# A state-space layer and a binarised MLP on one core: the scan's channels interleaved in pairs, smaller buffers, sums in groups of the array, and new transfer durations in the planner

## The chip, the cores and the metric

The kernel runs on 1 core of one Trainium2 chip. The time is that of the device, in microseconds (us), from the start of the program to its end. A profile is one more execution, with its own time. The engines of the core: PE multiplies matrices, DVE (VectorE) and POOL (GpSimd) work element by element, ACT (ScalarE) computes functions and copies, SP issues nearly all transfers. All five run their own instruction queue in order and wait for each other through semaphores.

## The reference, cut to what matters

Eight images x of 384 channels and 1024 positions go through a state-space block; then an MLP with weights reduced to signs is added. All is float32.

```python
t = layernorm(layernorm(x))                     # over channels
xm, z = split(t @ in_proj_w.T)                  # 768 channels each
xc = silu(causal_conv3(xm) + conv_b)
dt, Bm, Cm = split(xc @ x_proj_w.T, [24, 40])   # ranks 24, 16, 16
dt = softplus(dt @ dt_proj_w.T + dt_proj_b)
dA = exp(dt * A)                                # 16 states a channel
h[l] = dA[l] * h[l-1] + dt[l] * xc[l] * Bm[l]   # along 1024 positions
y = (sum over states of h * Cm) + xc * D
t = (y * silu(z)) @ out_proj_w.T
x = x + gelu(t @ mlp_w1.T + mlp_b1) @ mlp_w2.T + mlp_b2
# then, with sign-reduced W1, W2 and a clip per group of images:
x = x + quant(gelu(quant(layernorm(x) @ sign(W1))) @ sign(W2))
```

The last step quantises per group of one image for the first five images; for the other three it contributes zero, so they skip it.

## The kernel before, in words

Every operation is first written down in a `Plan` (L163), with its engine, a duration in us, what it reads and writes, and a priority; `run` (L221) then emits them one by one. It simulates the five engines, takes the engine that can start first, and there the operation of the best `rank` (L256) whose buffers are free. The order of each engine's queue, and so of all transfers on SP, comes from these durations. For a transfer, L332 to L334 reckon one shared stream: 1.0 us after the issue, 395 KB a us, and 0.9 us until it has landed. Where PE would be idle for more than 0.7 us (L312), `fill` (L412) issues filler products into the tile "spare", which compute nothing. Buffers come from rings (L369 to L386), one tag each, with a fixed number of tiles.

`s1` (L598) makes, image by image and in two halves of 512 positions, xc (p_in, L648), the product dbc with dt's 24 rows and B and C (p_dbc, L690; it yields two partial sums that lie on partitions 0 to 63 and 64 to 127), B and C added up and stored (p_bc, L701 to L716), dt in six products of the full array (p_dt, L722), softplus in one instruction over 3072 elements, dt times xc on POOL (L732), and z. xc, z, dt and dtx go to DRAM, each with one store of 1.5 MB a half, because the scan needs each channel on four partitions, one for each of four states.

`scan` (L761) takes 12 units an image. A unit has two tiles of 32 channels by four states and 1024 positions, and four quads of states. The first and the last image are scanned in halves, so a tile there is twice 512. For every tile and quad, `scan_tile` (L870) lets ACT compute da = exp(dt * A) into PSUM, POOL multiply dtx by B into u (L886), DVE run the recurrence (L890), and either POOL (L904) or DVE (L907) multiply by C; `on_pool` (L866) gives POOL 11 of 24 tiles. PE then adds the four states of a channel with a matrix of 32 columns, `fold`; four such products with outputs on four groups of 32 partitions make one slot of the array (L842). The result, gated by z, goes to DRAM.

`s3` (L912) does the out projection and the first MLP (p_out, p_h, p_o); gelu runs over 3072 elements at a time. `ffn` (L1092) is the second MLP (p_y twice), with the hidden layer stored and loaded again for the maximum that its clip needs. `binarise` (L988) reduces W1 and W2 to signs once, near the start; its means come from 21 products with a matrix of ones (p_sums, L1018). `mlp_out` (L977) takes the hidden layer in two parts of six chunks. For the last image `s3` follows the scan at once, with yg kept on chip.

Of the kernel before, what the change touches and what calls it, by code (L numbers as in the profile page):

```python
# [26 lines left out]
F32 = mybir.dt.float32  # L27
# [6 lines left out]
P = 128  # L34
# [8 lines left out]
HK = KH // 2  # L43
T = 512
# [42 lines left out]
def c_act(n):  # L87
    return 0.25 + n * 0.00084
# [5 lines left out]

def c_pool(n):
    return 0.18 + n * 0.00214
# [33 lines left out]
class Piece:  # L130
# [8 lines left out]

    def __getitem__(self, part):  # L140
        return self, part

# [13 lines left out]
class Op:  # L156
    __slots__ = (
        "engine", "cost", "emit", "prio", "slack", "table", "size",
        "wants", "next", "ready", "tiles", "others", "settle",
# [3 lines left out]
class Plan:  # L163
# [12 lines left out]
    def add(self, engine, cost, emit, r=(), w=(), claim=(), table=None, size=0, others=None):  # L176
# [3 lines left out]
        op.size, op.prio = size, (*self.prio, len(self.ops))  # L180
# [40 lines left out]
    def run(self):  # L221
# [60 lines left out]
        while left:  # L282
# [49 lines left out]
            if e == "SP":  # L332
                dma_free = max(dma_free, end + 1.0) + op.size / 395e3
                end = dma_free + 0.9  # L334
# [17 lines left out]
class Layer:  # L352
    def __init__(self, ctx, tc, a, out):
# [9 lines left out]
        def ring(tag, bufs, where=sbuf):  # L363
# [7 lines left out]
            "front": ring("front", 2), "t_f": ring("t_f", 2), "w_f": ring("w_f", 3),  # L371
            "dbc": ring("dbc", 1), "halo": ring("halo", 2),

            "dt_r": ring("dt_r", 3), "dtx_r": ring("dtx_r", 3), "u": ring("u", 9),
# [4 lines left out]
            "yg": ring("yg", 1), "hid": ring("hid", 2), "t_b": ring("t_b", 1), "w_b": ring("w_b", 3),  # L379
            "w6": ring("w6", 2), "w6_n": ring("w6_n", 2), "res": ring("res", 2),  # L380

            "t_n": ring("t_n", 2), "small": ring("small", 7),
# [9 lines left out]
        for b in range(B):  # L392
            for name in ("dt", "dtx"):
                self.dram[name, b] = handed(f"{name}_d{b}", [DI, L])
# [24 lines left out]

    def constants(self):
# [13 lines left out]
        self.pick = const.tile([P, 2 * NS], F32, name="pick")  # L436
        nc.vector.tensor_add(self.pick, ident[:, DQ : 2 * DQ], ident[:, DP + DQ : DP + 2 * DQ])
        self.edge = const.tile([P, KD, 2], F32, name="edge")
# [23 lines left out]
    def load(self, to, view, src, r=(), size=0, cost=0.4):  # L462

        self.plan.add(
            "SP", cost, lambda: self.nc.sync.dma_start(view(to.real), src), r=r, w=[to],
            size=size,
        )

    def store(self, dst, frm, view, w, size, cost=0.4):
# [6 lines left out]
    def rows_moved(self, t, parts, move, r, w):  # L476
        n = P // len(parts)
        for i, mem in enumerate(parts):
            self.plan.add(
                "SP", 0.35, lambda i=i, mem=mem: move(t.real[i * n : (i + 1) * n, :], mem),  # L480
# [3 lines left out]
    def weights(self, ring, k, src, r=()):  # L484
        w = self.piece(ring, [P, k, P], ring)
        self.load(w, lambda t: t, src, r=r, size=4 * P * k * P, cost=0.34)
        return w

    def matmuls(self, p, w, t, k0, n, start, stop, r, claim, w0=0):


        def emit():
            for k in range(n):
                self.nc.tensor.matmul(  # L494
                    p.real, w.real[:, w0 + k, :], t.real[:, k0 + k, :],
# [776 lines left out]
```

## Time and profile before

| what | us |
|---|---|
| median of 3 runs (lowest, highest) | 3261.21 (3260.56, 3263.69) |
| the profiled execution | 3262.23 |
| its span, first to last instruction | 3260.4 |
| mean clock granted to PE | 0.984 of full |
| busy: PE, DVE, ACT, POOL | 3122.5, 2742.3, 2024.3, 2848.7 |
| transfers | 748.73 MB, 230 GB/s |

In the lists, a row is a group of equal instructions: line, engine, operation, output and inputs by name, shapes and count, then the busy time of the group (overlaps counted once), the mean duration of one in ns, and the idle time of the engine just before them with what ended most of it. A float32 product shows as two matrix records, so 1152 records are 576 products. In rows of waits come the total, the number of times and the longest. In rows of stretches come the stretch and its length, then for PE, its weight loads, DVE, ACT and POOL the busy time and number of records, then the clock, the share of the transfer engines and GB/s.

### The profile page before, as it was taken

To read this page: it belongs to the slowest core of one execution; us is meant where nothing else is said; L and a number is where in the kernel's file an instruction comes from. 1 tells how busy PE (TensorE), PEld (TensorE's weight loads), DVE (VectorE), ACT (ScalarE), POOL (GpSimd) and SP (SyncE) were. 2 spreads that over 40 slices of the span, in tenths; PEclk is the share of its full clock that TensorE was granted. 3 is DMA by queue.
4 is the path that set the end of the run, shared out by engine and by line. 5 is a ranking of instruction groups with operands and counts; after the bars stand their busy time and mean duration, and the time that the engine had idled before them with its cause. 6 is when DMAs were issued, how large, how long until landed. Compare 5 with 4: busy or idle time off the path is not lost.

```text
span 3260.4 us, 34027 instructions
## 1 busy us (share of the span) xinstructions
PE 3122.5 (96%) x11098; PEld 1317.7 (40%) x11098; DVE 2742.3 (84%) x2127; ACT 2024.3 (62%) x2246; POOL 2848.7 (87%) x1371
## 2 busy tenths in 40 slices
PE   8988999999999999999899999999999999999999
PEld 4333433444433434334334344343443534433334
DVE  4778899799978899888998878999788988789880
ACT  4778787656665576665656566755666565656551
POOL 1688899979999989999989999989999899999970
PEclk9998999999999999999999999999999999999999
DMA  6988778657796568675686667866677656766542
GB/s 218 305 282 276 249 250 294 221 183 234 259 322 197 184 230 291 229 238 197 208 298 211 237 211 246 295 225 226 220 275 250 207 185 205 249 187 207 167 141 76
DMA packets 367345, 748.73 MB, mean 230 GB/s; under 512 B 33856, under 2 KB 111168, under 8 KB 367168
## 3 DMA queue, kind: packets, MB, share of 16 engines
q1 hardware_dynamic: 366736, 746.46, 68.5%
q8 instruction: 89, 1.46, 0.2%
q14 instruction: 88, 0.72, 0.1%
q10 hardware_dynamic: 432, 0.09, 0.0%
HBM read 566.06 MB, written 180.36 MB: 229 GB/s over the span
## 4 chain that ended last, share of the span: by engine, by line
PE 74%; DMA 9%; DVE 6%; ACT 5%; issue 2%; POOL 2%; SPq 1%; ACTq 0%; DVEq 0%; POOLq 0%
PE p_y L494 17%; PE p_o L494 14%; PE p_h L494 13%; PE py L842 9%; PE p_out L494 6%; PE p_z L494 6%; PE p_in L494 5%; DVE da L890 2%; DMA w<-in_out_proj_w 2%; DMA w_f<-in_in_proj_w 2%; DVE u L890 1%; ACT L510 1%; DMA w_b<-in_mlp_w 1%; ACT da L510 1%; PE spare L412 1%
## 5 line engine op out<-in xcount | busy, mean ns | idle before, releaser
L886 POOL TENSOR_TENSOR u<-dtx_r,bc 128x1024 f32<-128x1024 f32 x768 | 1790.4, 2362 | 72.3 <-DMA dtx_r<-dtx_d 46.3
L510 ACT ACTIVATE da<-dt_r,a_neg 128x1024 f32<-128x1024 f32 (+1 forms) x960 | 902.7, 945 | 534.0 <-DVE u L907 331.1
L904 POOL TENSOR_TENSOR u<-u,bc 128x1024 f32<-128x1024 f32 x352 | 828.4, 2364 | 121.5 <-DVE u L890 115.5
L890 DVE TENSOR_TENSOR_SCAN da<-da,u 128x1024 f32<-128x1024 f32 (+1 forms) x416 | 840.5, 2020 | 111.6 <-POOL u L886 62.9
L890 DVE TENSOR_TENSOR_SCAN u<-da,u 128x1024 f32<-128x1024 f32 (+1 forms) x352 | 699.5, 2010 | 90.3 <-ACT da L510 63.0
L494 PE MATMUL p_h<-t,w_b 128*128 128x512 f32 x1152 | 513.6, 600 | 10.9 <-DMA w_b<-in_mlp_w 9.9
L907 DVE TENSOR_TENSOR u<-da,bc 128x1024 f32<-128x1024 f32 x416 | 507.9, 1221 | 10.5 <-ACT state L901 0.3
L494 PE MATMUL p_o<-g,w 128*128 128x512 f32 x1152 | 506.7, 595 | 5.4 <-ACT g L510 2.9
L842 PE MATMUL py<-u,fold 128*32 128x512 f32 x3072 | 376.6, 605 | 4.5 <-DVE u L907 4.5
L494 PEld LDWEIGHTS p_h<-t,w_b 128*128 128x128 f32 x1152 | 214.7, 190 | 298.1 <-issue 256.4
L494 PEld LDWEIGHTS p_o<-g,w 128*128 128x128 f32 x1152 | 215.9, 190 | 292.0 <-issue 277.3
L494 PE MATMUL p_y<-tn,w_b 128*128 128x512 f32 x720 | 324.9, 598 | 4.0 <-DVE tn L592 3.3
L494 PE MATMUL p_y<-gf,w_n 128*128 128x512 f32 x720 | 319.0, 599 | 6.7 <-DMA w_n<-bin_w 4.0
L510 ACT ACT_TABLE_LOAD x222 | 284.8, 1283 | 11.7 <-DVE xc L661 7.3
L494 PE MATMUL p_out<-yg,w 128*128 128x512 f32 x552 | 249.2, 604 | 8.9 <-DMA w<-in_out_proj_w 4.3
L494 PE MATMUL p_z<-t,w_f 128*128 128x512 f32 x504 | 232.5, 611 | 8.2 <-DMA w_f<-in_in_proj_w 6.2
L494 PE MATMUL p_in<-t,w_f 128*128 128x512 f32 x504 | 228.3, 602 | 10.8 <-DMA w_f<-in_in_proj_w 8.6
L494 PEld LDWEIGHTS p_y<-gf,w_n 128*128 128x128 f32 x720 | 135.1, 191 | 187.6 <-issue 172.4
L494 PEld LDWEIGHTS p_y<-tn,w_b 128*128 128x128 f32 x720 | 133.9, 190 | 183.9 <-issue 155.4
L842 PEld LDWEIGHTS py<-u,fold 128*32 128x32 f32 x3072 | 81.5, 110 | 261.1 <-issue 203.2
L525 ACT ACTIVATE g<-p_h,v_vecs 128x512 f32<-128x512 f32 x157 | 106.3, 681 | 120.9 <-PE p_h L494 120.7
L525 ACT ACTIVATE y<-p_y,v_vecs 128x512 f32<-128x512 f32 x138 | 94.1, 683 | 130.0 <-PE p_y L494 100.3
(112 smaller groups left out, 2700.3 us busy)
## 6 DMA issues: line engine op xcount, KB each, us to landing
dtx_r<-dtx_d SPq DMA_DIRECT2D x144, 512.0 KB, 5.8
dt_r<-dt_d SPq DMA_DIRECT2D x144, 512.0 KB, 6.0
w_b<-in_mlp_w SPq DMA_DIRECT2D x192, 192.0 KB, 2.9
w<-in_mlp_w SPq DMA_DIRECT2D x96, 384.0 KB, 3.6
w_f<-in_in_proj_w SPq DMA_DIRECT2D x168, 192.0 KB, 4.2
y_d<-y SPq DMA_DIRECT2D x120, 256.0 KB, 3.4
gf<-y_d SPq DMA_DIRECT2D x20, 1536.0 KB, 9.5
xc_d<-xc SPq DMA_DIRECT2D x16, 1536.0 KB, 7.3
```

What stands on the lines that cost most here:

```text
L412: self.plan.fill = lambda: self.nc.tensor.matmul(self.plan.spare.real[:, : 2 * P], self.ones, self.one.to_broadcast([P, 2 * P]), start=Tru ...
L494: self.nc.tensor.matmul(p.real, w.real[:, w0 + k, :], t.real[:, k0 + k, :], start=start and k == 0, stop=stop and k == n - 1,)
L510: lambda: self.nc.scalar.activation(out(), in_(), func, **{k: v() if callable(v) else v for k, v in kw.items()}),
L525: nc.scalar.activation(out(), in_(), AF.Identity, bias=bias, scale=scale)
L842: nc.tensor.matmul(py.real[p0 : p0 + DQ, :], self.fold, hc, start=False, stop=(q == NQUAD - 1), skip_group_check=True,)
L886: add("POOL", 2.36, lambda: nc.gpsimd.tensor_mul(u.real, dtx_r.real, spread(bq)), r=[dtx_r, bq], w=[u])
L890: add("DVE", (0.2 if half else 0.15) + n * 0.00209, lambda k=k, col=col: nc.vector.tensor_tensor_scan(to.real[:, k, :], da.real[:, k, :], ...
L904: add("POOL", 2.36, lambda: nc.gpsimd.tensor_mul(u.real, u.real, spread(cq)), r=[cq], w=[u])
L907: add("DVE", 1.21, lambda: nc.vector.tensor_mul(u.real, da.real, spread(cq)), r=[da, cq], w=[u])
```

## The change

- **Pairs.** A scan unit holds two groups of 32 channels whose elements alternate in memory, [position, channel of the pair]. `scan_tile` becomes `scan_pair`: one POOL product for both channels of a pair, with the row of B or C repeated within a pair of elements (step 0), recurrences that read and write every second element, and fold products that do so too. s1 makes dtx interleaved (three POOL products a half instead of six) and stores it so; one load brings both channels. `on_pool` now decides for pairs: quads 0 and 2 always, quad 1 in every fourth unit, 27 of 48 pairs. In the last quad u takes the place of dtx. The ring of u has three pairs instead of nine tiles, that of dtx two pairs instead of three tiles. The assignment of channels to partitions (`_laid_out`) follows.
- **Pieces of two chunks.** xc, z, dt, yg and the hidden layers are `Split` into pieces of 2 x 512 elements with buffers of their own; silu, softplus, gelu, clips, stores and loads go piece by piece, and `mlp_out` emits its products two at a time. The first piece of an in-place function waits for all parts.
- **Sums in groups of the array.** One product with a matrix `join` adds dbc's two partial sums and puts dt's rows on partitions 0 to 31 and again on 32 to 63, B and C behind them; it is evicted into dbc. dt's products then run in twos, on rows 0 to 31 and 32 to 63 of the array, into two PSUM tiles. B and C leave with one store instead of four. In `binarise` the sums of three or four chunks go to separate groups of 32 output partitions.
- **Durations.** The planner's stream of transfers starts 0.5 us after the issue, moves 360 KB a us with 0.05 us each, and lands 1.5 us (weights), 2.3 us (other loads) or 1.6 us (the rest) later; issues are booked at 0.37 to 0.57 us.

The core of the diff:

```diff
+def c_pair(n):
+    return 0.19 + n * 0.00188
...
+class Split:
+
+
+    def __init__(self, make, n, per):
+        self.pieces, self.per = [make() for _ in range(n // per)], per
+
+    def at(self, k):
+        return self.pieces[k // self.per].real[:, k % self.per, :]
+
+    def __getitem__(self, k):
+        return self.pieces[k // self.per][k % self.per]
...
-                dma_free = max(dma_free, end + 1.0) + op.size / 395e3
-                end = dma_free + 0.9
+                dma_free = max(dma_free, end + 0.5) + 0.05 + op.size / 360e3
+                end = dma_free + op.land
...
-            "front": ring("front", 2), "t_f": ring("t_f", 2), "w_f": ring("w_f", 3),
...
+            "front": ring("front", 7), "t_f": ring("t_f", 2), "w_f": ring("w_f", 3),
...
-            "dt_r": ring("dt_r", 3), "dtx_r": ring("dtx_r", 3), "u": ring("u", 9),
+            "dt_r": ring("dt_r", 3), "dtx_r": ring("dtx_r", 2), "u": ring("u", 3),
...
-            "yg": ring("yg", 1), "hid": ring("hid", 2), "t_b": ring("t_b", 1), "w_b": ring("w_b", 3),
...
+            "yg": ring("yg", 3), "hid": ring("hid", 6), "t_b": ring("t_b", 1), "w_b": ring("w_b", 3),
...
+        self.join = const.tile([P, DP + 2 * NS], F32, name="join")
+        nc.vector.memset(self.join, 0.0)
+        for at, of, k in ((0, 0, R), (DQ, 0, R), (DP, DQ, 2 * NS)):
+            nc.vector.tensor_add(
+                self.join[:, at : at + k], ident[:, of : of + k], ident[:, DP + of : DP + of + k]
+            )
...
+        def in_place(t, func, table):
+            parts = [t[k] for k in range(KD)]
+            for p, piece in enumerate(t.pieces):
+                mine = parts[p * PER : (p + 1) * PER]
+                self.act(lambda piece=piece: piece.real, lambda piece=piece: piece.real, func,
+                         c_act(PER * T), r=parts if p == 0 else mine, w=mine, table=table)
...
-            def both_halves(dbc=dbc, p_bc=p_bc):
-                for g in range(G):
-                    nc.tensor.matmul(
-                        p_bc.real[g * DQ : (g + 1) * DQ, :], self.pick,
-                        dbc.real[:, g * TG : (g + 1) * TG], start=True, stop=True,
-                    )
...
+            p_all = self.piece("mm", [P, T], "p_all")
+            n_all = DP + 2 * NS
+            add("PE", MM, lambda dbc=dbc, p_all=p_all: nc.tensor.matmul(
+                p_all.real[:n_all, :], self.join, dbc.real, start=True, stop=True
+            ), r=[dbc], w=[p_all])
...
-                pd = self.piece("mm", [P, T], "p_dt")
-                add("PE", MM, lambda k=k, pd=pd, dbc=dbc, w=w: nc.tensor.matmul(
-                    pd.real, w.real[:, k % KC, :], dbc.real, start=True, stop=True,
-                ), r=[dbc, w], w=[pd], claim=[dt])
...
+                pds = [self.piece("mm", [P, T], "p_dt") for _ in range(2)]
+
+                def two(k=k, pds=pds, dbc=dbc, ws=ws):
+                    for i in range(2):
+                        rows = slice(i * DQ, (i + 1) * DQ)
+                        nc.tensor.matmul(
+                            pds[i].real, ws[i].real[rows, (k + i) % KC, :], dbc.real[rows, :],
+                            start=True, stop=True,
+                        )
+
+                add("PE", MM + 0.2, two, r=[dbc, *dict.fromkeys(ws)], w=pds, claim=[dt.pieces[k // PER]])
...
-            for k in range(KD):
-                add("POOL", c_pool(T), lambda k=k, xc=xc, dt=dt: nc.gpsimd.tensor_mul(
-                    xc.real[:, k, :], xc.real[:, k, :], dt.real[:, k, :]
-                ), r=[dt[k]], w=[xc[k]])
...
+            for p in range(KC):
+                dtx = self.piece("sq", [P, T, 2], "dtx")
+                add("POOL", 2.35, lambda p=p, dtx=dtx, xc=xc, dt=dt: nc.gpsimd.tensor_mul(
+                    dtx.real.rearrange("p n i -> p i n"), xc.pieces[p].real, dt.pieces[p].real
+                ), r=[xc[2 * p], xc[2 * p + 1], dt[2 * p], dt[2 * p + 1]], w=[dtx])
+                self.store(d.real[p, :, half * L : (half + 1) * L], dtx,
+                           lambda x: x.rearrange("p n i -> p (n i)"), [d[p, half]], 4 * P * L)
...
+            dtxs = self.piece("dtx_r", [P, wide, n, 2], "dtx_r")
+            d = self.dram["dtx", b]
+            at = 2 * cols.start
+            for x in range(wide):
+                src = d.real[p, r0 + x :: G, at : at + 2 * n].unsqueeze(1)
+                load(dtxs[x], lambda x=x, t=dtxs: t.real[:, x].rearrange("p n i -> p (n i)"),
+                     src.to_broadcast([DQ, SQ, 2 * n]), [d[p, h] for h in halves], 8 * P * n)
...
+                u = dtxs if q == NQUAD - 1 else self.piece("u", [P, wide, n, 2], "u")
+                self.scan_pair(
+                    u, [[(k * G + g) * NQUAD + q for k, g in groups] for groups in tiles],
+                    n, dts, dtxs, b_q[q], c_q[q], state, half, self.on_pool(q, m),
+                )
...
-                        parts = [
-                            (h * DP + i * DQ, hc.real[:, 0, HALVES[h]])
-                            for i, hc in enumerate(hcs) for h in both
-                        ] if half is None else [
-                            ((2 * i + k) * DQ, hc.real[:, k, :])
-                            for i, hc in enumerate(hcs) for k in both
-                        ]
...
+                        parts = [u.real[:, 0, h, i] for i in both for h in HALVES] if (
+                            half is None) else [u.real[:, x, :, i] for i in both for x in both]
...
-        return q == 0 or (q == 2 and (i == 0 or m % 3))
...
+    def on_pool(self, q, m):
+
+        return q % 2 == 0 or (q == 1 and m % 4 == 0)
...
-        add("POOL", 2.36, lambda: nc.gpsimd.tensor_mul(u.real, dtx_r.real, spread(bq)),
-            r=[dtx_r, bq], w=[u])
...
+    def scan_pair(self, u, cols, n, dts, dtxs, bq, cq, state, half, on_pool):
+
+
         nc, add = self.nc, self.plan.add
-        wide = len(cols)
-        da, u = self.piece("da", [P, wide, n], "da"), self.piece("u", [P, wide, n], "u")
...
+        def product(t, x, row):
+            nc.gpsimd.tensor_mul(
+                u.real[:, x], t.real[:, x], row.real.unsqueeze(2).to_broadcast([P, n, 2])
             )
...
+        for x in range(wide):
+            add("POOL", c_pair(2 * n), lambda x=x: product(dtxs, x, bq), r=[dtxs[x], bq],
+                w=parts[x])
+        for t, mine in enumerate(cols):
+            da = self.piece("da", [P, wide, n], "da")
+            dt_r = dts[t]
+            for i, col in enumerate(mine):
+                self.act(
+                    lambda i=i, da=da: da.real[:, i, :],
+                    lambda i=i, dt_r=dt_r: dt_r.real[:, i, :], AF.Exp,
+                    0.26 + n * 0.00084, r=[dt_r[i]], w=[da], table="exp",
+                    scale=self.a_neg[:, col : col + 1],
+                )
+
...
+            def in_u(i, t=t):
+                return u.real[:, 0, :, t] if wide == 1 else u.real[:, t, :, i]
+
+            to = (lambda i: in_u(i)) if on_pool else (
+                lambda i, da=da: da.real[:, i, :])
+            for i, col in enumerate(mine):
+                add("DVE", (0.2 if half else 0.15) + n * 0.00209, lambda i=i, col=col, to=to,
+                    da=da, in_u=in_u: nc.vector.tensor_tensor_scan(
+                        to(i), da.real[:, i, :], in_u(i),
+                        state.real[:, col : col + 1] if half else 0.0, ALU.mult, ALU.add,
+                    ), r=[da, u[t]] + ([state[col]] if half else []),
+                    w=[u[t] if on_pool else da])
+            if half == 0:
...
+                def by_dve(t=t, da=da):
+                    row = cq.real.unsqueeze(1)
+                    if wide == 1:
+                        nc.vector.tensor_mul(u.real[:, 0, :, t], da.real[:, 0, :], cq.real)
+                    else:
+                        nc.vector.tensor_mul(
+                            u.real[:, t].rearrange("p n i -> p i n"), da.real,
+                            row.to_broadcast([P, wide, n]),
+                        )
...
-            if on_pool:
...
+            for x in range(wide):
+                add("POOL", c_pair(2 * n), lambda x=x: product(u, x, cq), r=[cq], w=parts[x])
...
                     nc.tensor.matmul(
-                        pm.real, self.ones, w.real[:, k - ks.start, :],
-                        start=(k == 0), stop=(k == kt - 1),
+                        pm.real[g * DQ : (g + 1) * DQ, :], self.ones[:, :DQ],
+                        w.real[:, k - ks.start, :], start=(k < lanes), stop=(k >= kt - lanes),
                     )
 
-            add("PE", (ks.stop - ks.start) * MM, total, r=[w], w=[pm])
```

## The prediction

> **What bounds the kernel now.** I read the busy shares first, then the slices, then the costliest groups, then the waits, then busy time by stretch.
>
> ```profile
> PE 3122.5 (96%) x11098; PEld 1317.7 (40%) x11098; DVE 2742.3 (84%) x2127; ACT 2024.3 (62%) x2246; POOL 2848.7 (87%) x1371
> ...
> PE   8988999999999999999899999999999999999999
> ...
> DVE  4778899799978899888998878999788988789880
> ...
> POOL 1688899979999989999989999989999899999970
> ```
>
> The matrix engine PE is busy nearly everywhere; POOL and DVE, which carry the scan, run from the second slice to the last but one. So two resources are near their limit. The tail, once the scan is over, is PE alone. The groups that matter:
>
> ```profile
> L886 POOL TENSOR_TENSOR u<-dtx_r,bc 128x1024 f32<-128x1024 f32 x768 | 1790.4, 2362 | 72.3 <-DMA dtx_r<-dtx_d 46.3
> L904 POOL TENSOR_TENSOR u<-u,bc 128x1024 f32<-128x1024 f32 x352 | 828.4, 2364 | 121.5 <-DVE u L890 115.5
> L907 DVE TENSOR_TENSOR u<-da,bc 128x1024 f32<-128x1024 f32 x416 | 507.9, 1221 | 10.5 <-ACT state L901 0.3
> L842 PE MATMUL py<-u,fold 128*32 128x512 f32 x3072 | 376.6, 605 | 4.5 <-DVE u L907 4.5
> ```
>
> ```profile
> L722 PE MATMUL p_dt<-dbc,w_f 128*128 128x512 f32 x168 | 81.9, 620 | 9.5 <-ACT dt L525 6.0 <-ACT rows L523 3.4
> L412 PE MATMUL spare<-small 128*128 128x256 f32 x314 | 80.0, 396 | 0.1
> L722 PE MATMUL p_dt<-dbc,w_b 128*128 128x512 f32 x24 | 11.4, 608 | 0.9 <-DVE xc L661 0.9
> L703 PE MATMUL p_bc<-dbc,pick 128*32 128x128 f32 x128 | 6.7, 281 | 2.0 <-ACT dbc L523 2.0
> ```
>
> "spare" computes nothing: it is filler that the planner puts where it finds no PE work. So PE's real work is 3122.5 - 80.0 = 3042.5 us, and 218 us of the span are filler or idle. By stretch (PE column: busy, records):
>
> ```profile
> 0.00:400.00 400.00, 355.80 (x1442) 157.77 (x1442) 295.56 (x306) 281.00 (x372) 268.02 (x179) 0.96 0.81 265
> 400.00:3160.00 2760.00, 2670.25 (x9413) 1118.47 (x9410) 2429.45 (x1806) 1722.99 (x1852) 2575.98 (x1191) 0.99 0.69 230
> 3160.00:3260.40 100.40, 96.50 (x249) 41.47 (x247) 17.31 (x17) 20.27 (x23) 4.75 (x3) 1.00 0.26 81
> ```
>
> Filler in the three: 17.3, 62.0 and 0.6 us. Real PE work: 338.5, 2608.2, 95.9; loss (filler and idle): 61.5, 151.8, 4.5. In the middle, real PE work (2608) and POOL (2576) are 32 us apart in 2760: each at times holds up the other. PE's idle time there is spread thin:
>
> ```profile
> PE p_h L494 <- DMA w_b<-in_mlp_w: 9.9, 6, 2.8
> PE p_in L494 <- DMA w_f<-in_in_proj_w: 8.6, 6, 6.4
> ...
> PE p_dt L722 <- ACT dt L525: 6.0, 7, 3.2
> ```
>
> Waits on transfers come to 39 us of the middle's 90 us of idle; the rest are short waits on evictions and norms.
>
> [...] 1536 fold products of 32 columns (two records each) take 376.6 us, 0.98 us for four, against 93.3/96 = 0.97 us for one dt product. No row groups occur before. [...] 2364/1024 = 2.31 ns an element with two inputs, 0.94 with one (the clip at L1088, 2898 ns for 3072). [...] the interleaved pairs step exactly 8. [...] No run so far shows such steps.
>
> **The change part by part.**
>
> *PE.* (1) dt projection: 96 products of one slot (93.3 us) become 48 pairs on row groups 0 and 1, in separate banks. Low bound per pair 0.97 us (full overlap), high 1.94 (none). I take the fold's 0.98 and 0.06 for the switch: 50 us, so -43. (2) p_bc (6.7 us) goes; one 96-column product over 512 columns comes, 16 times, at the dt product's rate with a little start, 0.93: +8. (3) binarise's sums: 21 products, 18.7 us, become 6 slots of about 0.95, with two small products for the means: -12. Sum -47 us: real work 2995.5. Of it, by where those rows lie, -25 falls before 400 us (dt 36%, all of binarise) and -22 in the middle. The fold sums keep their number; they now read every second element. [...] +377 if a step of two halves the rate; I take 0. MLP products in pieces of two chunks are the same products.
>
> *POOL.* Products of tiles, 768 + 352 = 1120 at 2.36 us = 2619 us, become products of pairs: 384 for B, and for C 2.25 of four per unit and 96 units = 216; 600 in all. The row operand is now read with step 0 in the innermost place, each value for two elements. The trace has no such product. High bound: no saving, 2 x 2.362 = 4.72 us. Low: the second stream costs 2.31 - 0.94 = 1.37 ns an element, and halves: 1.63 x 2048 = 3.33 us. I take the middle, 4.03: 2418 us, -201. The rest cancels: dtx at L732 from six of 1.275 to three of 2.36 per half, -9; clips in thirds +2; the edge in six small operations instead of four +3; state copies +2. POOL: 2646.
>
> *DVE.* 416 multiplications by C become 384 x 2 - 216 x 2 = 336: -80 x 1.22 = -98 us, 2645. Scans keep number and length; [...] The other end is twice the scans' 1780 us (six rows of L890), with DVE as the bound; it goes with rival 5.
>
> *ACT.* In-place functions of 3072 (2.765 us) become three of 1024; from 2.765 and 1.476 (1536) the slope gives 1.05, so +0.37 each, 100 times: +37. The join eviction (0.57) replaces the smaller one (0.26): +5. ACT 2066, 63%: covered, since PE rarely waits for it; uncovered it would be 42 us. Table loads keep their number, since the first piece waits for all parts.
>
> *Queue of SP.* dtx loads 240 to 120 (twice the size); x, z and yg rows of the two split images +120; row stores 64 to 16; xc, z, dt, dtx stores 64 to 192; gf and yg loads 34 to 102. Net +148 issues of about 0.45 us, +67 us, on a queue whose own waits sum to over 1900 us: covered. Bytes are the same. The larger dtx buffer holds a pair twice over, where three single tiles did; its 46.3 us of POOL waits should shrink.
>
> *New waits.* dt products now wait for the join and its eviction, 0.93 + 0.57 = 1.5 us, 16 times: 0 to 24 us, since PE's queue is in order and everything behind stands; the planner puts other products between. A pair takes two of three PSUM buffers and needs 2 x 0.68 us of eviction per 1.04 of PE: 0 to 15 us. Together 9. The ring of u shrinks from nine tiles to three pairs, and the last quad works in dtx. A unit costs POOL 6.25 x 4.03 = 25 us; its first two buffers come free when the first sums are done, at about 17, the third at about 28, when it is needed at about 37: so nothing; if sums come late it is up to 2 us a unit, 192 us over 96 units, which POOL's slack (194 us, below) just covers.
>
> *Sum.* Before 400 us: 313.5 of work; DMA share is 0.81 there, bytes don't change, so I leave the loss: 375. Middle: work 2586; POOL's saving of 203 falls there by its share of POOL's work (2576/2849), 2576 - 184 = 2392, so the gap between the two grows from 32 to 194 us. Filler stands where PE had nothing because the scan was behind; I take three quarters away, 62 to 16. Idle: 90, less half of the waits on transfers (durations by kind, smaller pieces), plus 9: 79. Middle 2681. Tail 100.4, untouched. Span 3156.4; the profiled execution took 3262.2, 1.8 more than its span, and the median of the runs is 1 below it: 3157.
>
> **The rivals.**
> 1. *Only PE's own work goes.* The order is made anew, and the losses of 218 us return elsewhere. 3262.2 - 47 - 1 = 3214. For it: the 90 us of idle are many short waits. Against: filler is tied to the scan.
> 2. *POOL becomes the bound; slower.* If the stepless row operand is fetched per element, 600 x 4.72 = 2832, POOL 3060. It starts at 105 us, ends 91 before the end; with half of its present 228 us of waits in between: 105 + 3047 + 114 + 91 = 3357. It ends above today's time from 4.56 us a pair. For it: nothing in the trace shows the saving; more C products go to POOL. Against: the 0.94 with one input, which says the second stream is what costs.
> 3. *Row groups don't overlap*: 3157 + 43 = 3200.
> 4. *The middle loses almost nothing* (20 us instead of 95): 3082.
> 5. *Stepped reads slow the fold sums*: they cancel the gain from 28% (104/377); at twice the price it is 3157 + 377 = 3534.
>
> **How the numbers follow.** Forecast 0.60 (own range 3110 to 3195), rival 1 0.16, 2 0.07, 3 0.06, 4 0.08, 5 0.03. A measurement here tells 0.2% from no change. Faster: 0.60 + 0.16 + 0.06 + 0.08 = 0.90. Slower: rival 2 and two thirds of 5, 0.09; within 0.2%: 0.01. The range 3090 to 3230 leaves out rival 2, 5 and most of 4.
>
> **What would show it.** Right: pair products near 4.0 us; dt rows near 50 us; POOL busy near 2650, DVE near 2645; filler under 35 us in all; fold sums still near 377. Wrong: pair products over 4.5, fold means above 605 ns, dt rows near 93, or filler and idle again near 218.

## The result and the profile after

| | kernel before | changed kernel |
|---|---|---|
| median of 8 runs each, us (lowest, highest) | 3262.98 (3252.38, 3273.82) | 3255.03 (3245.19, 3258.27) |
| ratio, 95% interval | 1 | 0.9964 (0.9950 to 0.9978) |
| the profiled execution, us | 3262.23 | 3245.19 |
| its span, us | 3260.4 | 3243.2 |

The change makes the kernel 0.36% faster: 8 us where 104 were forecast, and outside the range. The profiled execution is the fastest of its eight, 10 us under their median.

First the busy shares and some of the 40 slices of the changed kernel:

```profile
PE 3105.3 (96%) x10920; PEld 1277.7 (39%) x10920; DVE 2666.2 (82%) x2091; ACT 2024.3 (62%) x2391; POOL 2728.5 (84%) x1031
...
PE   8878899999999999999999999999999999999999
...
DVE  4787889899788898878988789988788888787880
...
POOL 1888889988898978988889997889988899988980
PEclk9997999999999999999999999999999999999999
```

POOL lost 120 us and DVE 76, and 8's stand where 9's stood; PE lost 17 and is as full as before. Now PE's groups, equal shapes only:

```profile
L880 PE MATMUL py<-u,fold 128*32 128x512 f32 x2304 | 306.4, 628 | 5.1 <-POOL u L915 3.5 <-POOL w L1136 1.6
...
L880 PE MATMUL py<-dtx_r,fold 128*32 128x512 f32 x768 | 105.8, 611 | 1.4 <-DVE dtx_r L960 1.3
L434 PE MATMUL spare<-small 128*128 128x256 f32 x228 | 59.9, 399 | 0.5 <-DVE q L1163 0.3
L756 PE MATMUL p_dt<-dbc,w_f 32*128 32x512 f32 x168 | 58.8, 695 | 13.7 <-ACT rstd L539 8.3 <-ACT dbc L552 1.8 <-DVE t L621 1.7
...
L735 PE MATMUL p_all<-dbc,join 128*96 128x512 f32 x32 | 17.4, 627 | 7.6 <-ACT dbc L552 4.4 <-DVE xc L694 3.1
...
L756 PE MATMUL p_dt<-dbc,w_b 32*128 32x512 f32 x24 | 8.0, 641 | 0.0
```

Filler ("spare") fell from 80.0 to 59.9 us. But real work, 3105.3 - 59.9 = 3045.4, is what it was (3042.5). The fold sums, 376.6 us before in one group, are now 306.4 + 105.8 = 412.2, since the last quad reads dtx_r; their records grew from 605 to 628 and 611 ns. The two rows overlap in time; with each record counted from the end of the one before, the rise is 18 us. dt fell from 93.3 to 66.8, and "join" is new. POOL's groups:

```profile
L915 POOL TENSOR_TENSOR u<-dtx_r,bc 128x2048 f32<-128x2048 f32 x216 | 881.7, 4091 | 166.7 <-PE py L880 81.1 <-issue 72.7 <-DVE t L559 5.4
...
L915 POOL TENSOR_TENSOR u<-dtx_r,bc 128x1024 f32<-128x1024 f32 x144 | 304.4, 2135 | 23.5 <-PE py L880 11.3 <-DMA dtx_r<-dtx_d 9.0 <-issue 1.7
...
L1174 POOL TENSOR_SCALAR gf<-gf,q 128x1024 f32<-128x1024 f32 x60 | 70.8, 1198 | 2.5 <-DVE q L1167 2.5
```

A pair takes 4.09 us, a pair of halves 2 x 2.135 = 4.27. By stretch (the same cuts as before):

```profile
0.00:400.00 400.00, 334.08 (x1357) 138.65 (x1357) 292.88 (x321) 278.83 (x391) 276.36 (x188) 0.90 0.79 260
400.00:3160.00 2760.00, 2691.65 (x9367) 1104.53 (x9368) 2369.13 (x1765) 1729.04 (x1979) 2452.15 (x844) 0.99 0.70 232
3160.00:3260.00 100.00, 79.56 (x198) 34.53 (x196) 4.23 (x6) 16.39 (x21) 0.00 (x0) 0.99 0.21 64
```

Filler in the three is 11.5, 47.8 and 0.6 us. So PE's loss in the middle (filler and idle) fell from 151.8 to 2760 - 2691.65 + 47.8 = 116; at the start it rose from 61.5 to 77, at a granted clock of 0.90 instead of 0.96. Last, what PE and POOL waited for:

```profile
PE p_z L523 <- DMA w_f<-in_in_proj_w: 16.6, 11, 3.3
PE p_h L523 <- DMA w_b<-in_mlp_w: 8.5, 8, 2.0
PE p_dt L756 <- ACT rstd L539: 8.3, 1, 8.3
PE p_in L523 <- DMA w_f<-in_in_proj_w: 8.0, 3, 6.3
```

```profile
POOL u L915 <- PE py L880: 105.8, 45, 7.5
POOL u L915 <- DVE u L940: 83.2, 44, 9.5
POOL u L915 <- issue: 76.6, 20, 12.2
```

POOL waits 105.8 us for fold sums, 45 times: the ring of three pairs runs dry. Whether that costs anything is the first question. Two theories stood: (A) PE's own work sets the time and did not shrink, because the stepped reads of the fold sums and the join ate what dt gave; (B) the scan sets it, through POOL and its three buffers of u.

For the experiments I split PE's time in each profile: idle; filler; and real work, each record counted from the end of the one before it, with half the time of records of over one and a half times their usual length booked as "half clock". The trace's own record of the granted clock bears that name out: of 263 such records before and 265 in the changed kernel, 254 and 262 lie in stretches granted at 0.5 of full, and the others come before that record begins. Work, half clock, filler and idle make up the span, to within a few us. Two orders of the same work then compare:

| kernel | work at full clock | half clock | filler | idle | waits on transfers |
|---|---|---|---|---|---|
| before | 3007.7 | 40 | 75 | 134 | 56 |
| changed | 3003.6 | 46 | 56 | 134 | 50 |

By this count dt gave 27 us, the other sums of groups 11; the fold sums took 18, the join 10. Net 9, and rows whose products did not change took that back: they rose by 11, 9 of it at full clock.

### The profile page after: what moved, and what is told of

The parts are those of the page before. It is cut to its first block, busy times and chain, and to the rows that moved or that the text cites. A ratio compares the mean times of both kernels' runs of the same rounds, so it can differ in the third digit from the quotient of the medians.

```text
span 3243.2 us, 33719 instructions
## 1 busy us (share of the span) xinstructions
PE 3105.3 (96%) x10920; PEld 1277.7 (39%) x10920; DVE 2666.2 (82%) x2091; ACT 2024.3 (62%) x2391; POOL 2728.5 (84%) x1031
## 4 chain that ended last, share of the span: by engine, by line
PE 75%; DMA 9%; DVE 6%; ACT 4%; issue 2%; POOL 2%; SPq 1%; DVEq 0%; ACTq 0%; POOLq 0%
PE p_y L523 18%; PE p_o L523 14%; PE p_h L523 13%; PE py L880 9%; PE p_out L523 7%; PE p_in L523 5%; PE p_z L523 5%; DVE u L940 2%; DMA w_f<-in_in_proj_w 2%; DVE da L940 2%; DMA dtx_r<-dtx_d 2%; POOL u L915 2%; PE spare L434 1%; ACT da L539 1%; ACT L539 1%
## 5 line engine op out<-in xcount | busy, mean ns | idle before, releaser
L915 POOL TENSOR_TENSOR u<-dtx_r,bc 128x2048 f32<-128x2048 f32 (+1 forms) x360 | 1186.1, 3309 | 190.2 <-PE py L880 92.4
L915 POOL TENSOR_TENSOR u<-u,bc 128x2048 f32<-128x2048 f32 (+1 forms) x274 | 900.7, 3292 | 103.1 <-DVE u L940 81.8
L940 DVE TENSOR_TENSOR_SCAN u<-da,u 128x1024 f32<-128x1024 f32 (+1 forms) x436 | 868.2, 2006 | 113.9 <-ACT da L539 51.4
L940 DVE TENSOR_TENSOR_SCAN da<-da,dtx_r 128x1024 f32<-128x1024 f32 (+1 forms) x192 | 387.8, 2020 | 66.4 <-POOL dtx_r L915 38.2
L915 POOL TENSOR_TENSOR dtx_r<-dtx_r,bc 128x2048 f32<-128x2048 f32 (+1 forms) x120 | 396.4, 3309 | 1.6
L880 PE MATMUL py<-u,fold 128*32 128x512 f32 x2304 | 306.4, 628 | 5.1 <-POOL u L915 3.5
L940 DVE TENSOR_TENSOR_SCAN da<-da,u 128x1024 f32<-128x1024 f32 (+1 forms) x140 | 285.9, 2042 | 14.1 <-ACT da L539 10.3
L554 ACT ACTIVATE g<-p_h,v_vecs 128x512 f32<-128x512 f32 x146 | 99.6, 684 | 141.4 <-PE p_h L523 141.0
```

The lines of the kernel that those rows point to most:

```text
L554: nc.scalar.activation(out(), in_(), AF.Identity, bias=bias, scale=scale)
L880: nc.tensor.matmul(py.real[g * DQ : (g + 1) * DQ, :], self.fold, hc, start=False, stop=(q == NQUAD - 1), skip_group_check=True,)
L915: nc.gpsimd.tensor_mul(u.real[:, x], t.real[:, x], row.real.unsqueeze(2).to_broadcast([P, n, 2]))
L940: da=da, in_u=in_u: nc.vector.tensor_tensor_scan(to(i), da.real[:, i, :], in_u(i), state.real[:, col : col + 1] if half else 0.0, ALU.mult ...
```

## The experiments

Times are medians; ratios are to the kernel before in the same session, with their 95% intervals. The kernel before drifts by a few us between sessions, so differences between kernels are given by their ratios (0.001 is 3.3 us). Later expectations state their own theories, under the same letters.

**1. Fold sums that read 512 elements in a row.** The order stays; only the step goes.

```diff
-                        parts = [u.real[:, 0, h, i] for i in both for h in HALVES] if (
-                            half is None) else [u.real[:, x, :, i] for i in both for x in both]
+                        flat = [u.real[:, x].rearrange("p n i -> p (n i)") for x in range(wide)]
+                        parts = [f[:, j : j + T] for f in flat for j in range(0, 2 * n, T)]
```

> The changed kernel, in which the fold products read 512 neighbouring elements of the pair buffer instead of every second one: the same number of products of the same size, of other elements, so the two channels of a pair are mixed in y. Theory A (PE sets the pace; the stepped reads cost PE 18 us more in the fold, and the gain was eaten there): fold records back from 610 to 592 ns, the fold's share of PE time from 381 to 363 us, and the time 15 to 20 us below the changed kernel's 3255, so about 3237. Theory B (the ring of three pair buffers throttles the scan): the fold gets cheaper all the same, but the time stays within 5 us of 3255, since POOL still waits for buffers.

Measured: 3236.64 us, 0.9927 (0.9912 to 0.9941). Its fold groups:

```profile
L880 PE MATMUL py<-u,fold 128*32 128x512 f32 x2304 | 294.9, 609 | 4.4 <-POOL u L915 3.5 <-POOL w L1136 0.9
...
L880 PE MATMUL py<-dtx_r,fold 128*32 128x512 f32 x768 | 101.0, 592 | 2.5 <-DVE dtx_r L960 2.2 <-DVE dtx_r L962 0.3
```

Each record is 19 ns shorter (628 to 609, 611 to 592), the groups 16.3 us together, and the kernel is 12 us faster by the ratios, 18 by the medians. The stepped read has a price, and most or all of it reaches the time: as A had it, not B.

**2. No C products on POOL**, with a new order. **3. Less work for PE** (78 chunk products left out), with a new order. **4. A fourth buffer for u**, paid for by smaller rings elsewhere.

```diff
-        if on_pool:
-            for x in range(wide):
-                add("POOL", c_pair(2 * n), lambda x=x: product(u, x, cq), r=[cq], w=parts[x])
```

```diff
-                self.matmuls(po, w, g, i * HK + k, PER, i + k == 0, i * HK + k + PER == KH, need,
+                last = i * HK + k + PER == KH
+                self.matmuls(po, w, g, i * HK + k, PER - last, i + k == 0, last, need,
```

```diff
-            "front": ring("front", 7), "t_f": ring("t_f", 2), "w_f": ring("w_f", 3),
+            "front": ring("front", 6), "t_f": ring("t_f", 2), "w_f": ring("w_f", 3),
...
-            "dt_r": ring("dt_r", 3), "dtx_r": ring("dtx_r", 2), "u": ring("u", 3),
+            "dt_r": ring("dt_r", 3), "dtx_r": ring("dtx_r", 2), "u": ring("u", 4),
...
-            "w6": ring("w6", 2), "w6_n": ring("w6_n", 2), "res": ring("res", 4),
+            "w6": ring("w6", 2), "w6_n": ring("w6_n", 2), "res": ring("res", 2),
```

> The changed kernel without POOL's product by C (left out for 27 of 48 pairs; their sums are those of the state alone). POOL does about 900 us less, and the buffers come free earlier. Theory A: the time stays within 25 us of 3255 (only filler and some short waits go), POOL below 60%. Theory B: the scan runs ahead, PE's filler goes to nearly nothing and the time falls by 50 us or more.

> The changed kernel with one of twelve chunk products left out in every p_o and every second p_y product: 78 products fewer, about 78 x 0.88 = 69 us of PE. Theory A: the time falls by 55 to 75 us, to about 3190. Theory B: it falls by less than 35 us, and what PE saves shows as filler or idle time.

> The changed kernel with four pair buffers in the ring of u instead of three, paid for by one piece of front and two of res. Theory A: within 10 us of 3255; POOL's 106 us of waits on the fold shrink, and the time turns up in other waits of POOL. Theory B: POOL's waits on the fold fall below 40 us and the time falls by 25 us or more.

Measured: run 2, 3280.97 us, 1.0066 (1.0046 to 1.0085); run 3, 3210.84, 0.9843 (0.9827 to 0.9859); run 4, 3277.72, 1.0051 (1.0034 to 1.0068). In run 2 POOL is busy for 1840.9 us only, in run 4 its wait for fold sums falls from 105.8 to 72.9 us:

```profile
PE 3161.4 (96%) x11290; PEld 1339.3 (41%) x11290; DVE 2650.5 (81%) x2068; ACT 2019.4 (62%) x2401; POOL 1840.9 (56%) x759
```

```profile
POOL u L915 <- PE py L880: 72.9, 21, 7.2
```

The scan's last fold sum is done at 3030 us in run 2 and 3054 in run 4 instead of 3166. Yet both are slower than the changed kernel, by more than either theory had: filler is 137 and 120 us instead of 56, and when the scan is over, PE still has work of its own for 249 and 221 us, with under 6 us of filler and idle. In run 3 PE's work fell by 67 us and the time by 40, between the two forecasts; half clock and idle took the rest back. B gets no support: in these two orders a scan that is over more than 110 us sooner gained nothing. But the orders are new in all three, so one more run had to hold the order.

**5. The same order, C products of POOL over 8 positions only.** The planner books the old duration.

```diff
-                add("POOL", c_pair(2 * n), lambda x=x: product(u, x, cq), r=[cq], w=parts[x])
+                add("POOL", c_pair(2 * n), lambda x=x: nc.gpsimd.tensor_mul(
+                    u.real[:, x, :8], u.real[:, x, :8],
+                    cq.real[:, :8].unsqueeze(2).to_broadcast([P, 8, 2]),
+                ), r=[cq], w=parts[x])
```

> The changed kernel in exactly its own order of instructions, but POOL's product by C, 27 of 48 pairs, touches only 8 of 1024 positions (the sums of the rest are those of the state alone): some 800 us less of POOL with nothing moved. Theory A (PE's queue sets the pace, and what it loses lies in its own waits and filler): the time stays within 10 us of 3255. Theory B (PE is held up by the scan): it falls by over 25 us. If it stays, the 3281 of the run with re-planned order is an effect of order alone.

Measured: 3251.10 us, 0.9943 (0.9923 to 0.9963). Its page and POOL's groups:

```profile
PE 3115.9 (96%) x10920; PEld 1284.0 (40%) x10920; DVE 2666.4 (82%) x2091; ACT 2023.7 (62%) x2391; POOL 1891.8 (58%) x1031
```

```profile
L915 POOL TENSOR_TENSOR u<-dtx_r,bc 128x2048 f32<-128x2048 f32 x216 | 881.4, 4087 | 504.9 <-PE py L880 395.5 <-issue 92.9 <-DMA res<-in_x 5.8
...
L970 POOL TENSOR_TENSOR u<-u,bc 128x16 f32<-128x16 f32 x274 | 60.2, 220 | 346.4 <-DVE u L940 296.7 <-issue 24.0 <-PE py L880 19.8
```

POOL does 837 us less and hands all of it on as waiting, for PE (395.5) and DVE (296.7); the kernel gains 7 us by the ratios, 4 by the medians. In this order these 837 us of POOL's work held up next to nothing. The run can't speak of filler, which stands in PE's queue as before (57 us), nor of DVE, whose part of the scan stayed as it was. What PE itself waited for the scan's elements says the same: 4.5 us in the kernel before (the L842 row in the prediction) and at most 6.5 in the changed one (the two L880 rows above).

**6. dt pairs one after the other**: both products on rows 0 to 31, everything else the same.

```diff
-                        rows = slice(i * DQ, (i + 1) * DQ)
+                        rows = slice(0, DQ)
```

> The changed kernel in its own order, but both products of a dt pair use rows 0 to 31 of the array (the copy there is the same data), so they run one after the other. Theory A: a pair goes from 1.05 to about 1.75 us at full clock, 48 pairs, PE +34 us, and the time rises by 25 to 40 us, to about 3287. If the pairs were not on the path, the time stays within 8 us of 3255.

Measured: 3267.04 us, 1.0007 (0.9996 to 1.0019).

```profile
L756 PE MATMUL p_dt<-dbc,w_f 32*128 32x512 f32 x168 | 95.3, 687 | 12.9 <-ACT rstd L539 8.3 <-ACT dbc L552 1.8 <-DVE t L621 1.7
...
L756 PE MATMUL p_dt<-dbc,w_b 32*128 32x512 f32 x24 | 12.7, 643 | 0.0
```

dt takes 41 us more (66.8 to 108.0), so the row groups do overlap; but PE idles 24 us less (134 to 110), and the kernel loses 14 by the ratios, which neither theory had. Of what the overlap saves on PE, over half comes back as idle time. It doesn't come back ahead of the dt products themselves (13.7 us of idle with the overlap, 12.9 without). The largest part stands ahead of z's products, here in the changed kernel and in run 6:

```profile
L523 PE MATMUL p_z<-t,w_f 128*128 128x512 f32 x504 | 237.2, 620 | 20.2 <-DMA w_f<-in_in_proj_w 16.6 <-ACT dt L554 3.6
```

```profile
L523 PE MATMUL p_z<-t,w_f 128*128 128x512 f32 x504 | 235.1, 616 | 9.4 <-DMA w_f<-in_in_proj_w 9.3
```

**7, 8, 11, 12. Another order, nothing else.** The planner's durations of POOL's products (before) or of the pair product (changed) are moved by 1% or less, up as shown here or down by as much; the operations stay. (The slope 2.14 is that of POOL's shorter products and sums; the expectations of runs 16 and 17 call it the recurrence's, which was left alone.)

```diff
-    return 0.18 + n * 0.00214
+    return 0.18 + n * 0.00215
...
-        add("POOL", 2.36, lambda: nc.gpsimd.tensor_mul(u.real, dtx_r.real, spread(bq)),
+        add("POOL", 2.38, lambda: nc.gpsimd.tensor_mul(u.real, dtx_r.real, spread(bq)),
```

```diff
-    return 0.19 + n * 0.00188
+    return 0.19 + n * 0.00190
```

> The kernel before with the planner's duration of the POOL products at 2.38 instead of 2.36 us and the slope of the others at 2.15 instead of 2.14: no work is changed, only the order that the planner finds. If order is a matter of a few us, the time is within 5 us of 3262. If the planner's order is luck at the scale of this change, it moves by 10 us or more, either way.

> The changed kernel with the planner's slope of the pair products at 1.90 instead of 1.88 ns an element (measured: 1.91 at 4.09 us a pair): no work is changed, only the order. Within 5 us of 3255 if order hardly matters; off by 10 us or more if it is luck at the scale of this change.

> The changed kernel with the slope of the pair products at 1.86 instead of 1.88 ns: only the order changes. If order is luck, it is 10 us or more above 3255, since the changed kernel would be a favourable draw; if 1.90 was a freak, within 8 us of 3255.

> The kernel before with POOL products booked at 2.34 instead of 2.36 us and the slope at 2.13: only the order changes. If order is luck, 5 us or more above 3262 for the same reason, most likely 3270 to 3285; if not, within 5 us of 3262.

Measured: before, up 3279.57 us, 1.0039 (1.0025 to 1.0052), and down 3309.59, 1.0135 (1.0113 to 1.0158); changed, up 3289.53, 1.0057 (1.0036 to 1.0078), and down 3273.72, 1.0025 (1.0012 to 1.0038). PE's work at full clock stays within 7 us for each kernel; filler, idle and half clock move. A new order alone costs 13 and 44 us (before), 30 and 20 us (changed): more than the whole change gives. Each kernel as given is the fastest of its three orders.

**9, 10, 16, 17. The durations of transfers.** Run 9 takes them out of the changed kernel (issues stay booked as changed), in one order. Runs 10, 16 and 17 put all of them, issues too, into the kernel before, in three orders (as in 7 and 12).

```diff
-                dma_free = max(dma_free, end + 0.5) + 0.05 + op.size / 360e3
-                end = dma_free + op.land
+                dma_free = max(dma_free, end + 1.0) + op.size / 395e3
+                end = dma_free + 0.9
```

> The changed kernel with the stream of transfers in the planner as before (1.0 us, 395 KB a us, 0.9 us), issues booked as changed. If the new durations are what holds the changed kernel at its time, it is 15 us or more slower than 3255 and PE's waits on transfers grow from 45 to over 70 us. If order is luck at the scale of 15 to 35 us, as the two nudged runs say, it lies anywhere within 3245 to 3290 and the waits on transfers tell nothing clear.

> The kernel before with all of the planner's new durations of transfers and issues, and nothing else of the change. If these are worth what the forecast gave them, 20 us off PE's waits on transfers and about 3243. If they are only another order: between 3255 and 3285, PE's waits on transfers within 10 us of 45.

> The kernel before with the new durations of transfers (as in the run with all new durations, 3252.8 us), and the planner's POOL product 2.38 instead of 2.36 us, the recurrence's slope 2.15 instead of 2.14 ns. Theory A (the durations are what the change gains, and their gain is larger than the scatter of orders): the time stays below the kernel before, 3225 to 3260, PE's waits on transfers near 30 us. Theory B (the durations' run was a lucky order like others): 3265 to 3310, with filler and idle above 230 us.

> The kernel before with the new durations of transfers, and the planner's POOL product 2.34 instead of 2.36 us, the recurrence's slope 2.13 instead of 2.14 ns. With old durations these two numbers gave 3309.6. Theory A (durations matter beyond the scatter of orders): 3230 to 3275, at least 35 us below that run, PE's waits on transfers near 30 us. Theory B (luck of the order): 3280 to 3320.

Measured: run 9, 3313.29 us, 1.0144 (1.0120 to 1.0168); run 10, 3252.75, 0.9956 (0.9940 to 0.9971); run 16, 3261.58, 0.9984 (0.9968 to 0.9999); run 17, 3229.06, 0.9876 (0.9856 to 0.9897), the fastest of all that compute the whole. Run 9 fits the first case of its expectation, run 10 lies between its two; run 17 came out as A had it, run 16 just above A's range and below B's. PE's longest waits on transfers in run 9, then in run 10:

```profile
PE p_z L523 <- DMA w_f<-in_in_proj_w: 46.9, 16, 6.7
PE p_h L523 <- DMA w_b<-in_mlp_w: 17.1, 9, 3.9
```

```profile
PE p_h L495 <- DMA w_b<-in_mlp_w: 11.4, 10, 3.1
...
PE p_in L495 <- DMA w_f<-in_in_proj_w: 2.1, 2, 1.9
PE p_z L495 <- DMA w_f<-in_in_proj_w: 1.6, 2, 0.8
```

**13. The changed kernel with dt in six full-array products** and B and C as before. **14, 15, 18. The durations and the grouped sums of binarise in the kernel before**, in three orders.

```diff
-                add("PE", MM + 0.2, two, r=[dbc, *dict.fromkeys(ws)], w=pds, claim=[dt.pieces[k // PER]])
...
+                add("PE", MM, lambda k=k, pd=pd, dbc=dbc, w=w: nc.tensor.matmul(
+                    pd.real, w.real[:, k % KC, :], dbc.real, start=True, stop=True,
+                ), r=[dbc, w], w=[pd], claim=[dt.pieces[k // PER]])
```

> The changed kernel with dt in six products of the full array and the sums of B and C as before (no join, no row groups); pairs, pieces, grouped sums of binarise and durations stay. If the join's chain (product, eviction, product, eviction) is what slows the start, PE does over 168 us of work in the first 200 us; if it is the pieces or the pairs, it stays at 155 to 162. PE's work grows by about 16 us (dt 27 up, join 10 down). The time itself, with the scatter of orders: 3255 to 3290.

> The kernel before with the new durations and with binarise's sums in column groups, nothing else. PE's work is 12 us less, waits on transfers near 28 us as with the durations alone. If PE's work and these waits are what counts: 3253 - 12 = 3241, within the scatter of orders 3230 to 3270; start at 165 us of work or more in the first 200 us.

> The same with POOL products booked at 2.38 instead of 2.36 us: order alone. If the new durations make the planner's order reliable, within 8 us of e14; if order stays luck, 10 us or more from it.

> The kernel before with the new durations and the grouped sums of binarise (3255.0 us), and the planner's POOL product 2.34 instead of 2.36 us, slope 2.13 instead of 2.14. Theory A (durations matter beyond the scatter): 3220 to 3265. Theory B (luck of the order): 3270 to 3310.

Measured: run 13, 3295.89 us, 1.0102 (1.0069 to 1.0135); run 14, 3255.01, 0.9973 (0.9963 to 0.9983); run 15, 3231.38, 0.9901 (0.9867 to 0.9934); run 18, 3319.02, 1.0156 (1.0133 to 1.0178). Against runs 10, 16 and 17, order by order, the sums save PE 9, 4 and 10 us of work (3005.6 to 2996.7, 3003.9 to 2999.5, 3003.4 to 2993.3). The same two planner numbers gave the best order without the sums (run 17) and the worst of all with them (run 18, above B's range too), where filler alone is:

```profile
L413 PE MATMUL spare<-small 128*128 128x256 f32 x708 | 173.2, 392 | 2.8 <-DMA dt_r<-dt_d 1.8 <-DVE t L593 0.6 <-DVE tn L579 0.2
```

All orders by what they hold, three each, except the last two rows:

| kernels | ratios | idle | filler | half clock | waits on transfers |
|---|---|---|---|---|---|
| before (and 7, 12) | 1, 1.0039, 1.0135 | 134, 134, 151 | 75, 90, 100 | 40, 40, 46 | 56, 57, 78 |
| with durations (10, 16, 17) | 0.9956, 0.9984, 0.9876 | 102, 104, 102 | 113, 121, 91 | 28, 29, 29 | 28, 29, 19 |
| and sums (14, 15, 18) | 0.9973, 0.9901, 1.0156 | 105, 117, 122 | 122, 76, 166 | 27, 35, 40 | 26, 35, 35 |
| the change (and 8, 11) | 0.9964, 1.0057, 1.0025 | 134, 138, 138 | 56, 88, 88 | 46, 61, 51 | 50, 51, 46 |
| the change without durations (9) | 1.0144 | 176 | 67 | 69 | 90 |
| the change without dt pairs (13) | 1.0102 | 124 | 112 | 38 | 48 |

Idle time hardly depends on the order: 134 to 151 us in the kernel before without the durations, 102 to 122 with them, and its waits on transfers 56 to 78 and 19 to 35. That part works in every order tried. The rest of the change puts the idle time back to 134 to 138, and over all these orders filler goes from 56 to 166 us, with no pattern that the runs show. The mean ratios, 1.006, 0.994, 1.001 and 1.002, lie closer than the orders within a row, so which kernel is better over all orders isn't settled.

## Why the prediction was wrong

The span was forecast at 3156.4 and came at 3243.2. Two steps make the 87 us.

**Step "PE. Sum -47": measured +3 (3042.5 to 3045.4), a miss of 50.**
- The fold sums' reads were taken at 0, between 0 and +377: the author's estimate, which no trace then showed. They cost 18 by the trace, and run 1 gives 16 of it back: a record takes 605 ns before and 628 or 611 with the step on average, 592 and 609 at the shortest.
- dt: -27 instead of -43. The mechanism, row groups side by side, was right: counted from the end of the record before it, a pair at full clock takes 1.06 us (median; 1.91 in run 6), and 1.04 was forecast, 0.06 of it an estimate that no trace showed. But the rows sum to 66.8 us instead of 50. Nine of the 48 pairs touch stretches of half clock and take 20.5 us where nine at 1.04 would take 9.4; the term had no clock in it. The other 39 take 46.3 instead of 40.6.
- The join: +10, forecast +8 with p_bc's going taken in. The grouped sums: -11, forecast -12.
- The other 11 or so: products that did not change, 9 of it at full clock. The cause stays open.

**Step "Filler stands where PE had nothing because the scan was behind; I take three quarters away", and idle 90 to 79 in the middle: a miss of 37.** PE's loss was forecast at 161 us (61.5 + 95 + 4.5) and came at 198. The runs don't bear the premise out. In runs 2 and 4 the scan ends over 110 us sooner and filler rises to 137 and 120. In run 5 POOL is 837 us lighter and PE's idle time falls by 3 (134 to 131). That real PE work and POOL were 32 us apart in the middle was no sign of a second bound: PE waited 4.5 us for the scan's elements in the whole kernel before, which the prediction's own L842 row shows, and POOL, freed of work, waited for PE and DVE instead. Filler follows the order that the planner finds: with POOL's work unchanged, it is 56 to 88 us in three orders of the changed kernel.
- Idle: the durations did what was hoped, some 30 us off the idle time in every order tried. The rest of the change gives them back, where 9 us of "new waits" had been forecast. By run 6, 24 of it come with the overlap of the dt pairs; run 13 (124 us idle, one new order) has part of it. They don't come from the wait for two PSUM buffers that was forecast at 0 to 15, which would stand ahead of the dt products (10 us of idle there before, 14 after). Why z's products wait instead, and which pieces bring the rest, isn't settled.
- The start, left unchanged in the forecast, lost 16 us (61.5 to 77 in the first 400). The kernel before in its other two orders (runs 7 and 12) loses 72 and 77 there, so this may be order alone. In the first 200 us PE did 172 us of real work before, 157 after, 165 with dt as before (run 13) and 172 in run 14. Run 13 lies between the two signs that had been named for it, and its six dt products take PE longer by themselves. So how much of this is dt's chain stays open.

**Right:** DVE 2645 (2666), and its recurrences took nothing more for stepped operands, as the 2645 assumed without a trace that showed it (2283 ns against 2278, below). A pair product on POOL came at 4.09 us for 4.03, in part by luck: 4.03 was the middle of two bounds, and of the 0.63 us saved on two products of 2.362 the repeated operand gives 0.45 (2 x 2.135 = 4.27 at equal length) and one start fewer the rest (4.27 - 4.09 = 0.18), which the forecast didn't have. POOL's 2646 became 2728: the 0.06 a pair are 36 us, half-length pairs pay the start twice (4.27), and clips of 1024 took 1.20 us each, 70.8 in all against 57.9. Nothing hung on it. ACT's 2066 (2024) was too high. Of the signs of being wrong, fold means above 605 ns came, and filler and idle again near 218 nearly (198). Of the rivals, "only PE's own work goes" (3214) had the losses returning elsewhere, which they did; its -47 failed like the forecast's.

**What the measured 8 us are.** One order of each kernel was compared. Neighbouring orders of the changed kernel take 20 and 30 us more, of the kernel before 13 and 44. So the measured gain belongs to this pair of orders, and no part of the change can be credited with it.

## What to carry to other kernels

- A busy second engine beside a full first one is no second bound until its work is taken away, with the order held (for waits) and with a new order (for planned filler); do that, and read what the first engine waited for, before pricing a stall as its doing.
- Where a planner lays out the queues, try several orders of each version (nudge a duration by 1%): here three orders of one kernel lay 30 to 83 us apart, above most edits, and a good order with the new durations alone (run 17) gained 1.2%, where the change gave 0.4%.
- Follow a saving on the bounding engine into its waits: the overlapped dt pairs gave back over half of theirs (24 of 41 us), and not at the products themselves but at others (z's).
- Ask of every saving on PE whether the clock will be there: nine of 48 pairs met half clock, and cost 20.5 us, as much as twenty were forecast to.

## What the runs showed of the hardware

- A product whose moving operand takes every second float32 costs 19 ns more a record of 512 elements than one that reads a row (628 in the changed kernel against 609 in run 1, 611 against 592), 3%.
- Products on two row groups of 32 do run side by side: 108.0 us for 48 pairs one after the other (run 6), 66.8 together; at full clock 1.91 and 1.06 us a pair, counted from the end of the record before.
- A POOL product with one operand repeated in the innermost place takes 2135 / 1024 = 2.08 ns an element, against 2362 / 1024 = 2.31 with both read in step; at 2048 elements it is 4091 / 2048 = 2.00, with one start for both. With one input it is 2898 / 3072 = 0.94 (the clip of the kernel before), so the second adds 1.37; halving that would have saved 0.68, and at equal length a third of it came (0.22).
- A POOL operation with one input costs 2898 ns for 3072 elements but 1198 for 1024: splitting it in three adds 0.70 us.
- DVE's recurrence costs the same when it reads one input and writes its output at every second float32 (2283 ns for 1024 elements) as when all lie in a row (2278), here before and after:

```profile
L890 DVE TENSOR_TENSOR_SCAN u<-da,u 128x1024 f32<-128x1024 f32 x264 | 597.1, 2278 | 63.4 <-ACT da L510 41.4 <-POOL u L886 21.7
```

```profile
L940 DVE TENSOR_TENSOR_SCAN u<-da,u 128x1024 f32<-128x1024 f32 x324 | 738.7, 2283 | 80.9 <-POOL u L915 35.3 <-ACT da L539 34.5 <-POOL dtx_r L915 1.0
```
